# A two-layer transformer kernel: the first token tile of layer two is transposed inside layer one's last block, the routing's reads and first norm are tied to the projections, and the rope's buffers are doubled

## The chip, the core and the metric

One core of a Trainium2 chip runs the whole program in one launch. The metric is the device time of that launch in microseconds, median of several runs. The engines are named as in the profile: PE (TensorE, matrix products and transposes), DVE (VectorE), ACT (ScalarE), POOL (GpSimd) and SP (SyncE, which here only issues DMAs). Each engine works through its own queue in order, and semaphores tie the queues together. A stage's tiles live in SBUF, products in PSUM.

## The reference

2048 tokens of width 512, float32 throughout. Cut to what matters:

```python
xn = layernorm(x)
x  = x + linear_attention(xn) + moe_ffn(xn)       # layer one: 16 heads; 16 experts, top 8, dense
xn = layernorm(x)
x  = x + window_attention(xn) + depth_ffn(xn)     # layer two

def window_attention(x):          # 16 heads of 32, causal window of 1024
    q, k, v = split(x @ w_qkv)
    q, k = rope(rmsnorm(q) * q_gamma), rope(rmsnorm(k) * k_gamma)
    return softmax(mask(q @ k.T / sqrt(32))) @ v @ w_out

def depth_ffn(h):                 # only 256 of the 2048 tokens are processed
    scores = h @ w_router
    idx = sort(top_k(scores, 256))
    z = h[idx]                    # gather
    a = rms_norm(z) -> q, k, v (16 heads of 128) -> rope -> causal attention -> wo
    x1 = z + a
    y = x1 + silu(rms_norm(x1) @ w_gate) * (rms_norm(x1) @ w_up) @ w_down
    h[idx] = sigmoid(scores[idx]) * y + (1 - sigmoid(scores[idx])) * z
    return h
```

## The kernel before

A token tile is 128 tokens (16 of them, t = 0 to 15), a block is 512 tokens (b = 0 to 3).

**Layer one** runs the keys of all tiles, then four blocks of experts (about 141 us each). At the end of a block four groups `po` (seven products each, L515 to L518) give the layer's output for one token tile each; VectorE adds the residual (L519) and takes the layer norm's sums. In the last block each tile is normed at once by `normed`: xn goes to the DRAM tensor `xn_d`, the router's score to `score` (L98), xn plus x to `res_d`.

**The projections of layer two** (the `with ExitStack() as p4` stage) are the place of the change. For each token tile t:
- `turned(t)` takes xn of the tile, loaded two tiles ahead from `xn_d` into `xnq` (three buffers), transposes it on PE (`tr2`, L110) into PSUM, and ScalarE copies it to `xnt` (L117, three buffers). It is called for t + 1 after the first projection of tile t; tile 0's call stands just before the loop.
- three projections p0, p1, p2 (q, k, v) of four products each (L942), into three PSUM buffers;
- `normed_qk`: ScalarE squares p0 and p1 into `t1` (L740), VectorE sums to `rr` (L741), square root and reciprocal (L78, L79), VectorE scales to `qk` (L744), and POOL makes the rope: `t1 = qk*cos` (L749), `t2 = swapped qk*sin` (two halves, L754), `qk = t1 + t2` (L759). `t1` and `t2` have one buffer, `qk` two. The last tile's rope is on VectorE;
- `turned_qk`: PE transposes q and k of the tile before (`trqk`, L110), ScalarE copies into `qT`, VectorE into `kT`.

Between the products stand the steps of `maxima` (class `Steps`, `early`): score products `pa` (L593, with masks L599 and L601) of an earlier query tile into one PSUM buffer, which VectorE reduces at once (`mx`, L605); `tn` (L618) turns the finished maxima.

**The routing** finds the 256 largest scores while the projections run. It is a generator, `routing()`, and each `next(route, None)` in the projection loop runs it to its next `yield`. `largest` finds the threshold by counting: eight steps (h0 to h3, l0 to l3), each with POOL work `thr`, `ge` (L830 to L839), one small product `pc` on PE that sums over partitions (L843), ScalarE's copy `got`, and POOL work on it (L847 to L851):

```python
yield
pc = ps_t.tile([P, 15], F32, tag="tr", name=f"pc_{name}{k}")
PE.matmul(pc, ones, ge[:, :, 0], start=True, stop=True)
got = read(pc, f"got_{name}{k}")
yield
```

Then come two prefix sums (`ties`, `place`, products L878 to L881), and sixteen scatters of (token, score) pairs by indirect DMA from POOL's queue into four lists in DRAM (`list_d`, L911, four for each quarter; the indices `place` are in tiles that share the two buffers of `rr`). The lists were cleared before by four DMAs from a zeroed tile `lists`. Once tile 13 is in the program (`gathering`), POOL reads the four lists back, adds them, casts `idx` (L925) and issues four indirect DMAs that gather the rows `xs` and their rope table (`gather`, L674).

**The depth block** follows: `rms_norm_T(xs, 0, "a")` norms the gathered rows in two halves (`hn_a`: square on ScalarE L1001, scale on VectorE L1003, transposes `trh_a` on PE), and projections `k2p`, `v2p`, `q2p` follow, with weights streamed by SP. Then come its attention, its feed-forward net and, to the end, the window attention of layer two.

The order of instructions on each engine is not the order of the source lines: a scheduler builds each queue from the dependences and its own estimates. So an instruction of a later source line, such as hn_a, can stand early in a queue where its inputs are estimated to be there. The pools' buffers decide which tiles reuse which memory, and a tile waits for the last reader of what was there.

## Time and profile before

| | |
|---|---|
| runs | 1734.67, 1738.12, 1739.71 us; median 1738.12 |
| profiled execution | 1734.86 us, span 1733.2 us |
| instructions in the profile | 20487 |
| mean granted PE clock | 0.986 |
| PE, DVE, ACT, POOL busy | 1665.0, 966.0, 588.3, 532.7 us |
| keys of layer one, 0 to 150 us | PE busy 138.2 |
| experts, 150 to 696 | PE busy 545.7 |
| last po groups, 696 to 720.3 | PE busy 24.3 |
| projections and routing, 720.3 to 1045.5 | PE busy 282.4, POOL 174.8, DVE 180.3, granted clock 0.95 |
| depth block, 1045.5 to 1350 | PE busy 296.7 |
| window attention, 1350 to 1733 | PE busy 377.7 |

How to read it: "busy" is the time in which an engine had an instruction in work; a matmul in float32 leaves two rows in the trace. In a timeline row stand the start, the length, the engine, the line, the operation and tiles; in brackets the idle time of the engine before it, and what ended that. Tile names are shown without their numbers, so `t` is t1 or t2. In a row of busy time by stage stand the stretch, its length, the busy time of PE, PE's weight loads, DVE, ACT and POOL (each with its count), the granted PE clock as a share of full speed, the share of the DMA engines, and GB/s.

### The profile page before, as it was taken

The page shows a single profiled execution, that of the slowest core. Times are in us where ns is not written, and L with a number is a line of the kernel's source. Part 1 is how long each engine was busy: PE and PEld are TensorE (multiplying, and loading weights), DVE is VectorE, ACT ScalarE, POOL GpSimd, SP SyncE. Part 2 cuts the span into 40 slices and gives each one's busy share as a digit, 9 for nine tenths or more (in the row PEclk, how much of TensorE's full clock was granted, in tenths as well). Part 3 has the DMA queues.
Part 4 walks back from the last instruction along what each step waited for, and adds up shares of the span by engine and source line. Part 5 has one row for each costly group of instructions (what it writes and reads, how often), then busy time and mean ns, then how long its engine had stood idle before and what let it go on. Part 6 is the DMA issues. An engine that isn't in the chain of part 4 may idle for free.

```text
span 1733.2 us, 20487 instructions
## 1 busy us (share of the span) xinstructions
PE 1665.0 (96%) x8118; PEld 748.8 (43%) x8118; DVE 966.0 (56%) x1226; ACT 588.3 (34%) x947; POOL 532.7 (31%) x500
## 2 busy tenths in 40 slices
PE   8999999999999999988979989999999999999999
PEld 3445444444444444443434334454565333433333
DVE  4755646445344543335546676686555467567465
ACT  3313334333253254121111111242100566447473
POOL 3230000000000200178663333330000577558684
PEclk9999999999999999999989999999899999999999
DMA  9401001211031231310110005212132300110101
GB/s 358 169 33 46 25 31 36 74 54 31 18 116 57 54 115 37 63 47 25 25 40 25 13 20 204 99 50 73 47 116 65 114 2 1 50 50 1 50 1 37
DMA packets 61808, 107.11 MB, mean 62 GB/s; under 512 B 12208, under 2 KB 13744, under 8 KB 61200
## 3 DMA queue, kind: packets, MB, share of 16 engines
q1 hardware_dynamic: 55280, 104.01, 18.1%
q0 software_dynamic: 1152, 1.21, 0.5%
q10 hardware_dynamic: 5280, 0.59, 0.4%
q8 instruction: 63, 1.03, 0.2%
q14 instruction: 33, 0.27, 0.1%
HBM read 84.14 MB, written 21.65 MB: 61 GB/s over the span
## 4 chain that ended last, share of the span: by engine, by line
PE 80%; DVE 8%; POOL 5%; issue 2%; ACT 2%; DMA 2%; SPq 0%; POOLq 0%; DVEq 0%; ACTq 0%
PE ea L493 6%; PE eg L491 6%; PE acc L477 6%; PE ps L1271 6%; PE pa L593 6%; PE av L1345 5%; PE p L942 5%; PE po L515 3%; PE pq L366 3%; PE po L1315 3%; PE gx L241 3%; DVE mx L605 2%; PE mg L1185 2%; PE q2p L1017 2%; PE mu L1189 2%
## 5 line engine op out<-in xcount | busy, mean ns | idle before, releaser
L605 DVE TENSOR_REDUCE mx<-pa 128x4 f32<-128x1536 f32 (+3 forms) x144 | 253.1, 1757 | 157.6 <-PE pa L601 75.1
L1378 POOL TENSOR_TENSOR acc<-acc,pt 128x1024 f32<-128x1024 f32 (+2 forms) x110 | 252.6, 2325 | 95.7 <-DVE acc L1378 44.7
L1305 ACT ACTIVATE pt<-ps 128x1024 f32<-128x1024 f32 (+3 forms) x208 | 181.4, 924 | 107.9 <-PE ps L1294 61.6
L1378 DVE TENSOR_TENSOR acc<-acc,pt 128x1024 f32<-128x1024 f32 (+1 forms) x80 | 143.4, 1820 | 103.7 <-POOL acc L1378 103.7
L593 PE MATMUL pa<-kT,qT 32*128 32x384 f32 (+3 forms) x1152 | 139.3, 545 | 22.4 <-DVE mx L605 22.1
L349 ACT ACTIVATE r_e<-eg 128x512 f32<-128x512 f32 x128 | 75.8, 594 | 202.2 <-PE eg L491 194.4
L1271 PE MATMUL ps<-qT,kT 32*128 32x512 f32 (+3 forms) x1152 | 139.0, 525 | 0.0
L720 POOL TENSOR_TENSOR cosg<-cosg,gam 128x512 f32<-128x512 f32 x2 | 2.5, 1264 | 442.7 <-DVE gam L717 442.7
L942 PE MATMUL p<-w_qk,xnt 128*128 128x512 f32 x256 | 132.1, 639 | 3.9 <-ACT xnt L117 3.9
L351 DVE TENSOR_TENSOR h<-ea,r_e 128x512 f32<-128x512 f32 x128 | 87.3, 685 | 82.7 <-ACT r_e L350 82.2
L491 PE MATMUL eg<-xl,rwgT 128*128 128x512 f32 x256 | 130.8, 592 | 0.0
L493 PE MATMUL ea<-xw,rw1T 128*128 128x512 f32 x256 | 130.8, 592 | 0.0
L477 PE MATMUL acc<-h,rw2T 128*128 128x512 f32 x256 | 129.3, 592 | 0.0
L1345 PE MATMUL av<-pt,v 128*32 128x512 f32 (+3 forms) x1024 | 100.8, 482 | 0.0
L1271 PEld LDWEIGHTS ps<-qT,kT 32*128 32x128 f32 x1152 | 54.7, 183 | 93.8 <-issue 65.7
L593 PEld LDWEIGHTS pa<-kT,qT 32*128 32x128 f32 x1152 | 46.6, 187 | 105.4 <-DVE mx L605 67.2
L487 DVE TENSOR_TENSOR xw<-xw,xl 128x512 f32<-128x512 f32 x64 | 43.8, 686 | 84.9 <-DMA xw<-w_d 84.7
L350 ACT ACTIVATE r_e<-r_e 128x512 f32<-128x512 f32 x128 | 80.3, 629 | 5.6 <-ACT r_e L349 1.8
L491 PEld LDWEIGHTS eg<-xl,rwgT 128*128 128x128 f32 x256 | 48.7, 190 | 61.2 <-issue 60.5
L493 PEld LDWEIGHTS ea<-xw,rw1T 128*128 128x128 f32 x256 | 48.7, 190 | 61.2 <-issue 58.8
L477 PEld LDWEIGHTS acc<-h,rw2T 128*128 128x128 f32 x256 | 48.6, 190 | 61.2 <-issue 54.2
L942 PEld LDWEIGHTS p<-w_qk,xnt 128*128 128x128 f32 x256 | 46.4, 203 | 43.5 <-issue 39.5
(339 smaller groups left out, 2458.0 us busy)
## 6 DMA issues: line engine op xcount, KB each, us to landing
xw<-w_d SPq DMA_DIRECT2D x64, 256.0 KB, 3.3
x<-in_x SPq DMA_DIRECT2D x16, 256.0 KB, 4.5
res_d<-x SPq DMA_DIRECT2D x16, 256.0 KB, 3.5
xr<-res_d SPq DMA_DIRECT2D x16, 256.0 KB, 4.6
xn_d<-xn SPq DMA_DIRECT2D x16, 256.0 KB, 3.0
res_d<-xr SPq DMA_DIRECT2D x16, 256.0 KB, 3.3
xnq<-xn_d SPq DMA_DIRECT2D x16, 256.0 KB, 2.7
v_d<-vt SPq DMA_DIRECT2D x16, 256.0 KB, 2.0
```

Of the source, the lines that this page charges most:

```text
L350: S.activation(r, r, AF.Square)
L351: V.tensor_tensor(dst, pa, r, ALU.mult)
L477: PE.matmul(acc, rw2T[:, j, e, :], h, start=e == 0 and j == 0, stop=e == E - 1 and j == 1,)
L491: PE.matmul(pg, rwgT[:, e, hb], xl, start=True, stop=True)
L493: PE.matmul(pa, rw1T[:, e, hb], xw, start=True, stop=True)
L593: PE.matmul(pS[:, h, : w * P], qT[r, g, i * P : (i + 1) * P], kT[r, g, ks], start=True, stop=not (edge or last),)
L605: V.tensor_reduce(mx[:, g, :, c], pS[:, :, : w * P], AX.X, ALU.max)
L942: PE.matmul(pj, xnt[:, c, :], w, start=c == 0, stop=c == NC - 1)
L1271: PE.matmul(pS[h // 2][:, h % 2, t0 * P - q0 : (t1 + 1) * P - q0], kT[r, g, kb * P : (kb + 1) * P], qT[r, g, t0 * P : (t1 + 1) * P], start ...
L1305: S.activation(pT[:, :, :n], pS[hp][:, :, :n], AF.Exp)
L1345: PE.matmul(self.av[h * HD : (h + 1) * HD, t0 * P - o : (t1 + 1) * P - o], vs[kb // 4][:, kb % 4, hs], got[h // 2][:, h % 2, t0 * P - q0 : ...
L1378: eng.tensor_tensor(part, part, got[hp][:, :, : q1 - q0], ALU.add)
```

## The change

Five edits, all around the projections of layer two.

1. The pools for the projections' inputs (`w4`, `xq`, and a pool `xt4` of its own for `xnt`) are opened inside the last block of layer one, after the region of layer one's `xnT` is closed. `turned(0, ps, "mm")` is called there, ahead of the last token tile's po group, with a PSUM buffer of layer one.
2. `t1` and `t2` of the rope have two buffers each.
3. `next(route, None)` is called in the middle of each of the three projections and after each (six times for a tile, four before), and a count has one `yield` more between `ge` and its product.
4. The clearing DMAs read a small tile `empty`. `lists`, and two new small tiles `tok` and `nil`, are taken from the pool of `xnt`, so that each waits for the last reader of an older `xnt`: the list reads wait for tile 9's projections, the index (through `tok`) for tile 12's, and `zero` (through `nil`) for tile 13's.
5. The squares of `rms_norm_T` take `zero` as their bias.

```diff
-        xp = l0.enter_context(tc.tile_pool(name="xp", bufs=1, side="right"))
+        xp = xp_in.enter_context(tc.tile_pool(name="xp", bufs=1, side="right"))
...
+                if b == NTB - 1:
+                    xp_in.close()
+                    def pool(name, bufs):
+                        return p4.enter_context(
+                            tc.tile_pool(name=name, bufs=bufs, side="right", reuse_waits="tile")
+                        )
+                    w4, xq, xt4 = pool("w4", 1), pool("xq", 3), pool("xt4", 3)
...
+                    def turned(t, pool, tag):
+                        xn = xnq.pop(t)
+                        if t + 2 < NT:
+                            load_xn(t + 2)
+                        xnt = xt4.tile([P, NC, P], F32, tag="xnt", name=f"xnt_{t}")
+                        transpose4(
+                            pool, lambda c: xn[:, c * P : (c + 1) * P], xnt, f"tr2_{t}", scopy, tag
+                        )
+                        return xnt
+                    load_xn(0)
...
+                    load_xn(1)
...
+                    if t == NT - 1:
+                        xnt = turned(0, ps, "mm")
                     po = mm(f"po_{b}_{i}")
...
-            t1 = wka.tile([P, 2, HEADS, HD], F32, tag="t1", name=f"t1_{t}", bufs=1)
+            t1 = wka.tile([P, 2, HEADS, HD], F32, tag="t1", name=f"t1_{t}")
...
-            t2 = wka.tile([P, 2, HEADS, HD], F32, tag="t2", name=f"t2_{t}", bufs=1)
+            t2 = wka.tile([P, 2, HEADS, HD], F32, tag="t2", name=f"t2_{t}")
...
-            lists = const([P, 4, 2, 2], "lists", r5)
-            G.memset(lists, 0.0)
+            empty = const([P, 2, 2], "empty", r5)
+            G.memset(empty, 0.0)
...
                     yield
+                    yield
                     pc = ps_t.tile([P, 15], F32, tag="tr", name=f"pc_{name}{k}")
...
-            while not gathering:
+            while len(gathering) < 1:
                 yield
+            lists = xt4.tile([P, 4, 2, 2], F32, tag="xnt", name="lists")
...
-            G.tensor_copy(idx, listed[:, :, 0])
+            while len(gathering) < 2:
+                yield
+            tok = xt4.tile([P, 2], F32, tag="xnt", name="tok")
+            G.tensor_copy(tok, listed[:, :, 0])
+            G.tensor_copy(idx, tok)
...
+            while len(gathering) < 3:
+                yield
+            nil = xt4.tile([P, 1], F32, tag="xnt", name="nil")
+            G.memset(nil, 0.0)
+            G.tensor_copy(zero, nil)
             yield
...
-        xnt, last_qk = turned(0), None
+        last_qk = None
...
                     if c == 1:
                         early.some(t - 1)
-                        if j == 1 and t > 0:
+                        if t > 0:
                             next(route, None)
...
-                    next_xnt = turned(t + 1)
+                    next_xnt = turned(t + 1, ps_t, "tr")
+                    if t + 1 in (NT - 5, NT - 2, NT - 1):
+                        gathering.append(t)
...
-                S.activation(h, src[:, j, :], AF.Square, accum_out=ss)
+                S.activation(h, src[:, j, :], AF.Square, bias=zero, accum_out=ss)
```

The order of the queues that the two programs are built to differs in these places. PE: tr2 of tile 0 stands before the last po group; the counts pc of h1, h3, l1 and l3 stand at the end of p0 and no longer in the middle of p1, those of h0, h2, l0 and l2 in the middle of p2 and no longer at its end; ties stands before p2 of tile 5 and no longer after it, place at the end of p2 of tile 5 and no longer in the middle of p1 of tile 6. ACT and DVE: the first half of hn_a stands after the last trqk and no longer after tile 8. POOL: twelve scatters stand before the rope of tile 6 and no longer eight, the last four before the rope of tile 7 and no longer after it; the list reads follow the rope of tile 9 and no longer precede that of tile 8, the gather that of tile 12. SP: the loads of xnq for tiles 3 and 4 stand a few places earlier, and the biases `k2b` with the weights `k2w`, whose memory is now that of older q and k tiles.

## The prediction

> **What bounds the kernel now.** I read the page's first line, then the busy time by stage, then TensorE's waits inside the one stage that is not full.

> ```profile
> PE 1665.0 (96%) x8118; PEld 748.8 (43%) x8118; DVE 966.0 (56%) x1226; ACT 588.3 (34%) x947; POOL 532.7 (31%) x500
> 696.00:720.30 24.30, 24.30 (x59) 10.75 (x58) 9.34 (x27) 3.91 (x7) 0.00 (x0) 1.00 0.17 65
> 720.30:1045.50 325.20, 282.36 (x1328) 125.99 (x1326) 180.34 (x202) 58.86 (x123) 174.76 (x250) 0.95 0.14 35
> ```

> TensorE is the bound, and every edit lies around 720.3 to 1045.5, the projections of layer two. There it idles 325.2 - 282.4 = 42.8 us, at a granted clock of 0.95. Only idle time and clock there can be won. TensorE's timeline shows where (start, length, instruction, then the idle before it and who ended it):

> ```profile
> 724.60 5.40 PE L942 MATMUL p<-w_qk,xnt 128*128 128x512 f32 x8 [3.85 <-ACT xnt L117]
> 746.44 0.63 PE L110 MATMUL trqk<-ident,qk 128*128 128x128 f32 x4 [1.53 <-ACT xnt L117]
> 762.77 0.40 PE L843 MATMUL pc_h<-ge_h,ones 128*128 128x15 f32 x2 [3.56 <-POOL ge_h L839]
> 783.71 0.61 PE L843 MATMUL pc_h<-ge_h,ones 128*128 128x15 f32 x2 [2.84 <-POOL ge_h L839]
> 804.27 0.40 PE L843 MATMUL pc_l<-ge_l,ones 128*128 128x15 f32 x2 [1.77 <-POOL ge_l L839]
> 823.25 0.39 PE L843 MATMUL pc_l<-ge_l,ones 128*128 128x15 f32 x2 [2.25 <-POOL ge_l L839]
> 868.22 1.09 PE L110 MATMUL trqk<-ident,qk 128*128 128x128 f32 x4 [4.74 <-ACT xnt L117]
> 907.73 1.66 PE L593 MATMUL pa<-kT,qT 32*128 32x384 f32 x8 [8.23 <-DVE mx L605]
> ```

> Four of the eight are pc, the routing's count. The last names VectorE, but the chain of waits shows its origin, the gather of the chosen rows:

> ```profile
> 900.76 3.46 DMA xs<-xn_d,idx
> 904.24 0.73 ACT hn_a L1001 x2
> 905.52 0.49 DVE hn_a L1003
> ```

> hn_a, the norm of the gathered rows, stands in the ACT and DVE queues at token tile 8, so the projections' own work waits behind the gather.

> **A wait costs twice.** After 3.85 us of idle, eight rows of p took 5.40 us instead of 3.60 (as at 730.27): 1.8 more. The same comparison gives 1.9 after 3.56, 1.8 after 2.84, 2.0 after 2.25, 2.2 after 4.74, 2.7 after 8.23, and nothing after 1.53 and 1.77. So I add 2.0 to a wait above 2 us. [...]

> **Removed.**
> - Transpose of token tile 0 (tr2, then xnt's copy) now stands before the last po group. TensorE has something ready at 720.8: 3.85 + 1.8 = 5.65 us. Its four transposes (0.44) and ScalarE's copy (0.57) only move; ScalarE sits idle 3.95 us before 716.01, which covers the copy. The new t1 waits for the store of the last res_d rows (issued 724.10, landing 2.1 later); its second half needs p1 at 728.3, so nothing.
> - Two buffers for t1 and t2. ScalarE's squares no longer wait for POOL's rope of the tile before. The 1.53 at 746.44 becomes 0.5 (then rope itself is late): 1.0. The 4.74 at 868.22 has the same form: squares and xnt's copy wait for a rope held behind eight scatters. In the new order twelve scatters (1.27 us apart) precede that rope, which ends 28.3 us after the place matmul: 1.8 to the index copy, three trains of 5.1 with two starts of 0.8 and 0.5, one landing of 3.8 less 1.3, and 7.25 of rope. TensorE has 31.1 us of work and slow clock to issue first (28.6 from the rows 834.3 to 863.5, less the place itself, 0.45, and 2.0). So the wait is gone, 2.9 us in hand: 4.74 + 2.2 = 6.9.
> - hn_a behind the last tile: 8.23 + 2.7 = 10.9. Gather and list reads sit on POOL after ropes 12 and 9. Four list reads, landing and adds take about 7 us, gather with its copies 5.5; POOL is idle 9.66 us between ropes there (928.29 to 937.96), so neither delays a rope.

> Together 5.65 + 1.0 + 6.9 + 10.9 = 24.45 us.

> **Added: the counts come earlier in TensorE's queue.** The extra yields move each second count (h1, h3, l1, l3) from the middle of p1 to the end of p0. That is 1.72 us of p plus a transpose and a maxima step less ahead of it, and as much more behind it. TensorE issues in order, so a count that is early waits with everything behind it. The ring: count, rest of p1, squares to qk, rope, count chain, next such count. From POOL's timeline:

> ```profile
> 791.66 2.35 POOL L749 TENSOR_TENSOR t<-qk,cosg 128x1024 f32<-128x1024 f32 x1 [0.76 <-DVE qk L744]
> 793.98 2.51 POOL L754 TENSOR_TENSOR t<-qk,sing 128x512 f32<-128x512 f32 x2
> 796.56 2.35 POOL L759 TENSOR_TENSOR qk<-t,t 128x1024 f32<-128x1024 f32 x1
> 802.79 1.43 POOL L839 TENSOR_TENSOR ge_l<-ge_l 128x120 f32<-128x120 f32 x4
> ```

> From 791.66 to the count at 804.27 is 12.6 us; interleaved as in the new order 12.4. From p1's end to the rope's start is 4.35 (806.32 to 810.65). From count to p1's end is now 5.4 of work for l1 (p 3.6, transpose, one maxima step, the count) plus 2.0 of clock. Ring l1 to l3: 12.4 + 7.4 + 4.35 = 24.15, where it was 804.27 to 823.25 = 19.0. TensorE has 16.3 + 2.0 us in it, so it waits 5.85. Likewise h3 to l1: 12.4 + 8.2 + 4.35 = 24.95 against 19.9 of work: 5.0. h1 to h3: 9.6 to the next count, 0.7 to read it, 12.7 of chain and rope = 23.0 against 16.7: 6.3. For h1 the chain restarts at 742.6 and takes 10.1 with a rope in it; TensorE arrives at 749.2: 3.45. Last, the place matmul stands at the end of p2 and not in the middle of the next p1: l3 to place is 7.6 + 4.35 + 10.35 = 22.3 against 16.15: 6.15, where it waited nothing. Sum: 3.45 + 6.3 + 5.0 + 5.85 + 6.15 = 26.75, plus 1.9 + 4 x 2.0 of clock = 36.65. Before: 3.56 + 2.84 + 1.77 + 2.25 + 1.9 + 1.8 + 2.0 = 16.1. Added: 20.5.

> **At the end of the stage**, both halves of hn_a follow the last tile; the first meets the transposes and maxima there, 0.3. The first weight of the next stage now reuses memory that holds qk until the last trqk: it is issued at 1041.2, not 1038.17. With landings of 5.2 (q2w) to 6.3 (k2w) it arrives 0.3 to 1.4 after TensorE asks; a queued one (v2w, 9.8) would give 5. I take 0.6, so 0.9 for the end. The biases beside it, the small tile that resets the lists, the zero tile and its use as bias: nothing; POOL's gaps and the queue behind that weight hide them, at 0.2 each if not.

> **Sum**: -24.45 + 20.5 + 0.9 = -3.0. The profiled execution took 1734.86 (span 1733.2 and 1.7 around it), 3.3 under the median; on the median of 1738.1 that is 1735.1. The difference of two sums of 20 is not known better than about 6 us: five clock losses of 1.4 to 2.7 each, 1 us in each ring.

> **Rivals.**
> 1. *The counts wait no more than before.* If POOL or the copies around it run freer (rope no longer starts late in tile 2, the steps interleave), the 20.5 does not arise: -24.45 + 0.9 = -23.5; with the scatter wait of 6.9 kept, -16.7, or 1721.4. For it: POOL is idle 4.13 and 2.34 us before two of the old ropes. Against: 4.35 + 12.4 is a chain without slack.
> 2. *VectorE gets between.* In the rings the reduction of a maxima step (1.67 to 2.21 us) stands just ahead of rr, the sum that starts the rope. It ends about as p1 does. If it begins over 0.5 us late, it pushes the rope: up to 2.2 us in each of four rings, 8.8, with TensorE idle all of it: 1735.1 + 8.8 = 1743.9, slower.
> 3. *The handover isn't won.* Should the early transposes wait, or ScalarE's copy fall behind the norm of the last rows, 5.65 returns: 1740.8.

> **Chances.** Forecast 0.50, its own range 1729 to 1742: 0.14 of it below, 0.30 within and 0.06 above the 0.3% (5.2 us) that a measurement can tell from no change. Rival 1 0.27, faster. Rival 2 0.17, slower. Rival 3 0.06, 0.04 within and 0.02 slower. Faster 0.14 + 0.27 = 0.41, same 0.34, slower 0.25. The range goes from rival 1 with its scatter wait, less 1.4, to rival 2 plus 2.1: 1720 to 1746.

> **What would show it.** Right: no wait at the first p of tile 0; none at trqk of tile 6; hn_a after the last trqk and no DMA in front of a pa; waits of 5 to 6.5 us before pc_h, pc_l and place, and 23 to 25 us between them. Wrong: counts that wait under 3 us (rival 1), a pc released late because a rope began over 5 us after p1's end (rival 2), or a wait at k2p above 2 us.

## The result, and the profile after

| kernel | median us | ratio to before, 95% interval |
|---|---|---|
| before | 1735.45 (12 runs beside the change) | |
| changed | 1735.43 (12 runs) | 0.9998 [0.9989, 1.0007] |

No difference that can be measured. The profiled execution took 1737.09 us (span 1735.1, mean granted clock 0.985). The page's first line and two stages by the same cut as before:

```profile
PE 1668.9 (96%) x8118; PEld 750.4 (43%) x8118; DVE 965.6 (56%) x1226; ACT 589.8 (34%) x947; POOL 532.6 (31%) x503
696.00:720.30 24.30, 24.30 (x61) 10.97 (x60) 9.33 (x27) 4.50 (x8) 0.00 (x0) 1.00 0.21 76
720.30:1045.50 325.20, 285.95 (x1321) 127.70 (x1319) 179.41 (x201) 59.66 (x122) 174.52 (x253) 0.94 0.11 30
```

TensorE is busy 1668.9 us instead of 1665.0 with the same 8118 instructions, and idle 1735.1 - 1668.9 = 66.2 instead of 68.2. The idle time did fall, by 2.0; the same products took 3.9 longer. Most of that is the granted clock: half of TensorE's busy time inside the stage's stretches at half clock, which is what they cost (in the changed kernel four rows of p took 3.73 us at half clock, from 779.04, and 1.94 at full clock, from 784.17), is 13.3 us before and 16.2 now. This execution is the slowest of the changed kernel's 12, so the profiles differ by more (1.9 us of span) than the medians do (0.0). TensorE's timeline shows what became of the eight rows of before (start, length, then the idle time before it in brackets):

```profile
721.03 3.60 PE L968 MATMUL p<-w_qk,xnt 128*128 128x512 f32 x8
739.87 0.66 PE L110 MATMUL trqk<-ident,qk 128*128 128x128 f32 x4 [0.33 <-POOL qk L772]
752.36 0.40 PE L857 MATMUL pc_h<-ge_h,ones 128*128 128x15 f32 x2 [2.67 <-POOL ge_h L852]
774.74 0.61 PE L857 MATMUL pc_h<-ge_h,ones 128*128 128x15 f32 x2 [5.53 <-POOL ge_h L852]
802.51 0.61 PE L857 MATMUL pc_l<-ge_l,ones 128*128 128x15 f32 x2 [4.34 <-POOL ge_l L852]
827.37 0.61 PE L857 MATMUL pc_l<-ge_l,ones 128*128 128x15 f32 x2 [5.75 <-POOL ge_l L852]
844.94 0.40 PE L892 MATMUL place<-sel,after 128*128 128x16 f32 x2 [0.96 <-POOL sel L910]
849.35 0.61 PE L893 MATMUL place<-inc,ones 128*128 128x16 f32 x2 [4.01 <-POOL inc L889]
881.22 0.60 PE L110 MATMUL trqk<-ident,qk 128*128 128x128 f32 x4
1046.97 1.98 PE L1043 MATMUL k2p<-k2w,hT_a 128*128 128x512 f32 x4 [0.47 <-DMA k2w<-in_wk]
```

The first p of tile 0 has no wait in front (3.85 before), nor has trqk of tile 6 at 881.22 (4.74), and no gather stands before a pa (8.23). In their place the second counts and place wait 2.67 + 5.53 + 4.34 + 5.75 + 0.96 + 4.01 = 23.3 us, where the counts waited 10.4.

### The profile page after: what moved, and what is told of

Read it like the earlier page. It is cut to its first block, busy times and chain, and to the rows that moved or that the text cites. A ratio compares the mean times of both kernels' runs of the same rounds, so it can differ in the third digit from the quotient of the medians.

```text
span 1735.1 us, 20506 instructions
## 1 busy us (share of the span) xinstructions
PE 1668.9 (96%) x8118; PEld 750.4 (43%) x8118; DVE 965.6 (56%) x1226; ACT 589.8 (34%) x947; POOL 532.6 (31%) x503
## 4 chain that ended last, share of the span: by engine, by line
PE 81%; DVE 8%; POOL 4%; DMA 2%; issue 2%; ACT 2%; SPq 0%; DVEq 0%; POOLq 0%; ACTq 0%
PE ea L494 6%; PE acc L478 6%; PE eg L492 6%; PE p L968 6%; PE pa L632 6%; PE ps L1297 6%; PE av L1371 5%; PE po L553 3%; PE pq L367 3%; PE po L1341 3%; PE gx L242 3%; DVE mx L644 2%; PE mg L1211 2%; PE q2p L1043 2%; PE sg L403 2%
## 5 line engine op out<-in xcount | busy, mean ns | idle before, releaser
L288 PE MATMUL pk<-k_wT,xnT 128*128 128x512 f32 x128 | 61.6, 624 | 3.5 <-ACT xnT L117 3.5
```

## Experiments

All are timed beside before, in three groups, where its medians were 1736.96, 1736.02 and 1735.77 us. The differences told below are taken from the ratios (0.9893 is 0.0107 x 1736 = 18.6 us); some expectations name those of the medians, which are up to 1.5 us apart from them. Each kernel has one trace.

| kernel | edits in it | median us | ratio to before, 95% interval |
|---|---|---|---|
| early transposition alone | 1 | 1729.02 | 0.9963 [0.9949, 0.9976] |
| two buffers alone | 2 | 1723.41 | 0.9931 [0.9918, 0.9945] |
| cadence alone | 3 | 1758.42 | 1.0131 [1.0116, 1.0147] |
| ties alone | 4, 5 | 1725.40 | 0.9937 [0.9923, 0.9950] |
| edit 3 undone | 1, 2, 4, 5 | 1718.43 | 0.9893 [0.9877, 0.9910] |
| edit 2 undone | 1, 3, 4, 5 | 1738.82 | 1.0020 [1.0010, 1.0029] |
| ties undone | 1, 2, 3 | 1734.85 | 0.9995 [0.9986, 1.0004] |
| edits 1 and 2 | 1, 2 | 1716.16 | 0.9887 [0.9872, 0.9902] |
| waits filled | all, and filling | 1729.94 | 0.9964 [0.9950, 0.9978] |
| slow cadence | 1, 2, 4, 5, half of 3 | 1704.39 | 0.9815 [0.9801, 0.9828] |
| slow cadence, ties undone | 1, 2, half of 3 | 1704.34 | 0.9820 [0.9807, 0.9834] |
| slow cadence, even scatters | as slow cadence, and more | 1699.32 | 0.9790 [0.9777, 0.9804] |

**Edit 3 undone.** The question: did the counts take back what the rest won, or was nothing won?

```diff
-                        if t > 0:
+                        if j == 1 and t > 0:
                             next(route, None)
...
-                    yield
                     yield
                     pc = ps_t.tile([P, 15], F32, tag="tr", name=f"pc_{name}{k}")
```

> Changed kernel with edit 3 undone (one call of next in the middle of a tile's projections, not three; one yield before a count's product): edits 1, 2, 4 and 5 stand alone. Theory T (the counts' waits and the half clock behind them took back what the other edits won): in the trace of the changed kernel the second counts and place wait 2.67 + 5.53 + 4.34 + 5.75 + 0.96 + 4.01 = 23.3 us and the slow clock behind them takes about 14.3, where before had 16.1 in all; so 21.5 us go: 1735.4 - 21.5 = 1714, between 1709 and 1719, with waits of 1.5 to 4 us before pc and none before place. Rival R1 (nothing was won: TensorE idles in this stage for whatever comes late next, and the counts only took the place of other waits): 1731 to 1737, and waits of 20 us or more before other products. Rival R2 (the two-buffer rope or the gather isn't worth its part): 1720 to 1726.

It is 18.6 us faster than before, interval 15.6 to 21.4: R1 falls. TensorE's waits (us in total, times, longest):

```profile
PE pc_h L856 <- POOL ge_h L852: 6.1, 2, 3.5
PE pc_l L856 <- POOL ge_l L852: 4.1, 2, 2.3
PE trqk L110 <- POOL qk L772: 3.3, 2, 3.0
```

The counts wait 10.2 and place nothing. But 1718.4 is 4.4 above the 1714 expected: with the old cadence trqk of tile 6 still waits 3.0 us, now for the rope itself, behind eight scatters.

**Cadence alone** (edit 3 put into before).

> Kernel before with edit 3 alone (three calls of next in the middle of a tile's projections, two yields before a count's product). Theory T: the second counts come early and wait 23 to 27 us with 10 to 14 of slow clock behind, where they cost 16.1 before: +20.5 to +21.5; with one buffer for t1 and t2, twelve scatters instead of eight stand before the rope that the squares of the next tile wait for, at most 5 more: 1735.5 + 21 = 1756.5, between 1752 and 1763. Rival R1 (the stage has a fixed amount of idle time): 1733 to 1742, the waits of the gather and the scatters shrinking by what the counts wait more.

22.7 us slower, interval 20.1 to 25.5, as theory T has it. Its waits, and the pa behind the gather:

```profile
PE pc_l L844 <- POOL ge_l L839: 10.1, 2, 5.8
PE pc_h L844 <- POOL ge_h L839: 8.2, 2, 5.6
PE place L880 <- POOL inc L876: 4.0, 1, 4.0
913.77 1.67 PE L593 MATMUL pa<-kT,qT 32*128 32x384 f32 x8 [9.31 <-DVE mx L605]
```

The counts wait as in the changed kernel, and the gather's wait did not shrink to make room (9.31, it was 8.23). One thing was not expected: with single buffers and twelve scatters before the rope of tile 6 there is no wait at trqk of tile 6. Place stands earlier there, and TensorE has more to issue before that trqk; the next experiment but one tests whether the edit and not the buffers removes the wait.

**Early transposition alone** (edit 1).

> Changed kernel with edits 2, 3, 4 and 5 undone: the early transposition of tile 0 alone. Theory T: the idle 3.85 us before the first p of tile 0 and 1.8 of slow clock go, 5.65 in all: 1735.5 - 5.65 = 1729.9, between 1727.5 and 1732. Rival R3 (the first counts take it back: their chain starts at the last scores of layer one, so TensorE only reaches pc_h0 and pc_h1 earlier and waits there): within 1.5 us of 1735.5, with a wait of 6 us or more before pc_h1, where it was 3.56.

6.4 us faster, interval 4.2 to 8.9: R3 falls. The first p starts at once, and trqk of tile 6 still waits:

```profile
720.43 3.60 PE L956 MATMUL p<-w_qk,xnt 128*128 128x512 f32 x8
860.69 1.09 PE L110 MATMUL trqk<-ident,qk 128*128 128x128 f32 x4 [4.55 <-ACT xnt L117]
```

The wait before pc_h1 is the 3.56 us it was. Beyond the handover, two other waits are shorter: 2.28 before h3 (2.84) and 0.66 before l1 (1.77). Why these two shift a little from kernel to kernel wasn't followed up.

**Edit 2 undone, and two buffers alone.** Both change only `bufs=1` of t1 and t2.

> Changed kernel with edit 2 undone (one buffer each for t1 and t2), the rest as it is. The kernel with edit 3 alone has single buffers and yet no wait before trqk of tile 6, since place comes earlier there. Theory T2 (that wait is removed by edit 3, not by the buffers, which are worth only the 1.53 us before trqk of tile 0): 1735.4 + 1.2 = 1736.6, between 1735 and 1739, no wait before trqk of tile 6. Rival (the prediction's own ledger, buffers worth 1.0 + 6.9): 1743.3, with a wait of 3 us or more before trqk of tile 6.

> Kernel before with edit 2 alone (two buffers each for t1 and t2). Theory T2: with the old cadence the rope of tile 6 is itself late behind eight scatters; the kernel with edit 3 undone waits 2.98 us there for qk: 1.53 becomes 0.34 and 4.74 becomes 2.98, together 3.0, the slow clock behind the wait stays: 3 us faster than before, between 1.5 and 5. Rival (the prediction's own term): 7.9 faster, 6 or more, and no wait before trqk of tile 6.

Undone, it costs 0.22%, 3.8 us, against the changed kernel; neither 7.9 nor quite 1.2. Its rows show where:

```profile
740.89 0.63 PE L110 MATMUL trqk<-ident,qk 128*128 128x128 f32 x4 [1.53 <-ACT xnt L117]
756.34 1.11 PE L110 MATMUL tr<-ident,xnq 128*128 128x128 f32 x4 [2.15 <-ACT got_h L117]
884.08 0.63 PE L110 MATMUL trqk<-ident,qk 128*128 128x128 f32 x4 [0.88 <-ACT xnt L117]
```

Only 0.88 us at trqk of tile 6; but a wait of 2.15 behind the copy of a count, which no expectation had listed. ScalarE's queue holds that copy behind a square that waits for the rope (idle 9.82 us until POOL's qk):

```profile
755.62 0.60 ACT L753 ACTIVATE t<-p 128x512 f32<-128x512 f32 x1 [9.82 <-POOL qk L772]
756.12 0.17 ACT L117 COPY got_h<-pc_h 128x15 f32<-128x15 f32 x1
```

Alone, the two buffers bring 12.0 us (9.5 to 14.2) where 3 were expected. That was wrong by much, and the rows say why. The wait at tile 6 is still there, but the norm of the gathered rows has moved (second row, ScalarE):

```profile
866.11 0.66 PE L110 MATMUL trqk<-ident,qk 128*128 128x128 f32 x4 [3.60 <-POOL qk L759]
1028.55 0.63 ACT L1001 ACTIVATE hn_a<-xs 128x512 f32<-128x512 f32 x1
```

In before hn_a runs at 904.2, in the middle of tile 8's work. With two buffers the scheduler puts it behind the last tile, though no line of code asks for that, and the 8.23 us go with it. What in the scheduler's estimates moved it was not looked into.

**Ties alone, ties undone, edits 1 and 2.** So edits 2 and 4 may remove the same wait. Three kernels test that.

> Kernel before with edits 4 and 5 alone (the small tiles come from the buffers of xnt in its own pool). Theory T: the 8.23 us before the pa of tile 9 and 2.7 of slow clock go, 0.3 come back at the end of the stage: 10.6 faster than before, between 8.5 and 12.5; hn_a stands behind tile 15's xnt. Rival R6 (the wait only moves: the gather now ends behind tile 14, and rr of tile 14 or 15 waits behind hn_a): at most 6 faster, with a wait of 3 us or more before a pa or a trqk of tiles 14 and 15.

> Changed kernel with edits 4 and 5 undone (edits 1 to 3 stay). Edit 2 alone had already moved hn_a behind the last tile, with no wait before the pa of tile 9. Theory T3 (edits 2 and 4 each remove the same 8.23 + 2.7 us, so the second is worth nothing): within 2 us of the changed kernel, 1735.4, no wait above 3 us before a pa. Rival (the prediction's ledger, 10.9 by edits 4 and 5): 1746, a wait of 8 us before a pa near tile 9.

> Kernel before with edits 1 and 2 only (edits 3, 4 and 5 undone). Theory T3: the two alone moved the time by -7.9 and -12.6; the rope that is late behind the scatters stays, so their sum and the kernel with edit 3 undone (1718.4) should meet: 1717, between 1713 and 1720. Rival: edits 4 and 5 add 10.9 to it in the kernel with edit 3 undone, so without them 1725 to 1730.

Alone, the ties bring 10.9 us (8.7 to 13.4), hn_a's first half runs late, and no pa waits over 1.9 us (R6 falls):

```profile
998.03 0.72 ACT L1012 ACTIVATE hn_a<-xs,zero 128x512 f32<-128x512 f32 x1
```

Beside edit 2 they bring nothing: without them the changed kernel takes 1734.85 (ratio 0.9995, against 0.9998), and edits 1 and 2 alone (0.9887) do as well as edits 1, 2, 4 and 5 (0.9893). T3 holds: edits 1, 2 and 4 with 5 bring 6.4 + 12.0 + 10.9 = 29.3 us each by itself and 18.6 together, and the 10.7 between are the one wait that two of them remove.

**Waits filled.** Is the slow clock behind the waits caused by them?

```diff
-                    pc = ps_t.tile([P, 15], F32, tag="tr", name=f"pc_{name}{k}")
+                    pc = ps_t.tile([P, D], F32, tag="tr", name=f"pc_{name}{k}")
+                    for _ in range({'h1': 2, 'h3': 5, 'l1': 4, 'l3': 5}.get(f"{name}{k}", 0)):
+                        PE.matmul(pc, ident, w_v[:, 0, :], start=True, stop=True)
+                    pc = pc[:, 0:15]
```

(and four such products ahead of place).

> Changed kernel with idle time filled: ahead of the counts h1, h3, l1, l3 and of place stand 2, 5, 4, 5 and 4 products of 128x512 (0.86 us each) of ident with w_v, written to the count's own PSUM tile and overwritten by it. Theory T (the half clock behind the waits is caused by the idle time, and lengthens the rings themselves): the waits before these products fall from 23.3 to under 8 us in all, the granted clock between 740 and 860 us from 0.83 to 0.90 towards 1.0, and of the 14.3 us of slow clock 8 to 14 go, 1 to 3 us of the filling not covered: 1725, between 1720 and 1730. Rival R7 (the half clock comes of something else than TensorE's idle time): 1735 to 1745, clock as before, the filling partly added.

A kernel with 18.0 us of additional products is 0.34% faster, 5.9 us, than the changed kernel without them. Busy time and clock from 740 to 860 us, the changed kernel first, then this one:

```profile
740.00:860.00 120.00, 95.31 (x428) 45.54 (x429) 46.35 (x59) 19.48 (x44) 79.72 (x163) 0.86 0.07 20
740.00:860.00 120.00, 112.99 (x506) 52.57 (x504) 50.46 (x63) 21.39 (x47) 83.05 (x165) 0.97 0.10 23
```

The clock rises from 0.86 to 0.97 as the idle time falls from 24.7 to 7.0 us, and place is issued 7.5 us earlier (841.84 against 849.35). So the slow clock comes of the idle time (R7 falls), and it lengthened the rings: p1 stands in each of them. Of the 7.5 a new wait took back 3.1, and VectorE shows whose it is:

```profile
857.52 1.22 DVE L754 TENSOR_REDUCE rr<-t 128x32 f32<-128x1024 f32 x1 [3.35 <-DMA list_d<-tokc,place]
861.40 0.93 PE L632 MATMUL pa<-kT,qT 32*128 32x384 f32 x8 [3.10 <-DVE mx L644]
```

`place` shares the two buffers of rr, so rr of a tile waits until a scatter has read its indices, here 3.35 us.

**Slow cadence.** The calls of next as before (four for a tile), the two yields of the change kept. A count now takes three calls, so it stands one call further behind its `ge` than with edit 3 undone, and the counts come every 0.75 tile and not every half. The expectation's "1.33 tiles" has the fraction upside down.

> Changed kernel with the calls of next as before (four for a tile), but with the two yields before a count's product kept: a count comes every 1.33 tiles and not every half or whole one. Theory T: a ring from one count to the next is 22 to 28 us with a rope in it and about 10 without, and TensorE has 1.33 tiles, 24 us or more, of work between two counts: waits of under 3 us in all before pc and place, so that also the 16.1 us that the counts cost before go: 1714 - 13 = 1701, between 1696 and 1707; the gather comes some 40 us later, still ahead of the last tile's end. Rival R4 (POOL's queue, not the place of the counts, sets when they end; slower calls only move the waits): 1711 to 1718, like the kernel with edit 3 undone. Rival R5 (the later gather is late for hn_a): a wait of over 3 us before trh_a at the end of the stage.

> The kernel with four calls of next for a tile and two yields before a count's product (1704.4), with edits 4 and 5 undone: are they needed where the counts no longer wait? Theory T3: hn_a stays behind the last tile, nothing waits for the gather: 1704.4, between 1702 and 1707; two list reads now stand before the rope of tile 10 and two inside it, at most 2 us. Rival (they are needed): 1712 or more, with hn_a's gather ahead of a pa.

1704.4 with the ties and 1704.3 without: R4, R5 and the need for the ties fall. The counts' waits are down to 0.91 us in all. The time expected was met, but not for the reason given: there are 9.9 to 15.6 us between two counts and not 24. What the rows show is that `ge` is ready when TensorE arrives: POOL's last add of it ends 3.0 to 9.5 us before the product for h1, h3 and the four l counts, and only h2 waits. What is left is one rope late behind scatters, seen in POOL's rows and in TensorE's:

```profile
870.05 0.19 POOL L923 CAST place<-pos 128x4 int32<-128x4 f32 x1 [3.06 <-DMA list_d<-tokc,place]
875.51 2.37 POOL L762 TENSOR_TENSOR t<-qk,cosg 128x1024 f32<-128x1024 f32 x1
882.81 1.07 PE L110 MATMUL trqk<-ident,qk 128*128 128x128 f32 x4 [2.26 <-POOL qk L772]
```

**Slow cadence, even scatters.**

```diff
-                for _ in range(4):
+                for _ in range((6, 4, 3, 2)[n]):
                     yield
```

> The kernel with four calls of next for a tile and two yields before a count's product, and with 6, 4, 3 and 2 yields behind the four groups of scatters where each had 4. Four scatters then stand before the ropes of tiles 8, 9, 10 and 11 and not eight before that of tile 8; list reads and gather stay where they are. In the trace with 4 yields each the rope of tile 8 began 8.1 us later than its qk, after 3.06 us in which POOL waited for a scatter's landing, since place and rr share two buffers, and TensorE waited 2.26 us at trqk of tile 8, with 3.41 us of half clock behind. Theory T4: this wait and its slow clock go: 1704.4 - 4.0 = 1700.4, between 1698 and 1703. Rival R8 (the wait moves to a later tile, or into rr, whose buffers wait for later scatters): 1703 to 1707 with a wait of 2 us or more before a trqk or a pa of tiles 9 to 12.

1699.3, the fastest of all: 2.1% under before, interval 1.96 to 2.23%. T4 holds, R8 falls. The rope of tile 8 starts as soon as its qk is there, and the page gives the least busy time of any:

```profile
867.07 2.35 POOL L762 TENSOR_TENSOR t<-qk,cosg 128x1024 f32<-128x1024 f32 x1 [0.56 <-DVE qk L757]
PE 1654.2 (97%) x8118; PEld 744.3 (44%) x8118; DVE 965.4 (57%) x1226; ACT 589.2 (35%) x947; POOL 533.8 (31%) x503
```

## Why the prediction came out as it did

The time of 1735.43 lies 0.3 us from the 1735.1 forecast, but that is closer than the working was, and luck: it subtracted 3.0 from a median of 1738.12 out of three runs; beside the change before ran at 1735.45, and the change moved the time by 0.0. That two sums of over 20 us nearly cancel was right, though the chances put faster (0.41) above same (0.34). Of the two sums the traces and experiments say this:

- **Handover, 5.65.** Right: no wait at the first p, 6.4 [4.2, 8.9] alone, of which 1.7 are the two other waits that were shorter there. Rival 3 did not come.
- **Two buffers, 1.0 and 6.9.** In the changed kernel both waits are gone, as said (0.33 at tile 0 where 0.5 was predicted, none at tile 6). But the 6.9 was put down to the wrong edit. The earlier place matmul removes that wait, with single buffers too (0.88 left); two buffers under the old cadence leave 3.0 to 3.6 of it. The argument of 28.3 us of scatters and rope (its terms add up to 28.15) against 31.1 us of TensorE's work held, with less in hand: the rope ends 30.3 us after place's second product (849.35 to 879.69), and TensorE comes to trqk after 31.9 (881.22). In before it came there 19.6 us after place (843.84 to 863.48) and waited 4.74. The 31.1 came from the early place, which was booked as a cost alone.
- **Gather and hn_a, 10.9.** The size is right (10.9 alone), and it is gone. It could have been had from edit 2 alone, and so edits 4 and 5 are worth nothing here. The prediction compared the queues of before and after only, and these cannot tell which edit moved an instruction.
- **Counts, 26.75 of waits.** 23.3 measured: 2.67, 5.53, 4.34, 5.75 and 4.97 for 3.45, 6.3, 5.0, 5.85 and 6.15. Rivals 1 and 2 are out. The rings h1 to h3 and l1 to l3 came as predicted (22.4 and 24.9 for 23.0 and 24.15). Ring h3 to l1 took 27.8 and not 24.95: from h3 to the end of p1 TensorE needed 11.4 us instead of 8.2, at half clock, while rope and count took 12.2 (12.4 predicted). VectorE did not come between: in all four rings rr starts 0.7 us after p1's end, and the rope follows 4.2 us after it, but for the ring from h1 to h3, where POOL's own count chain holds it back (5.8).
- **Slow clock, 2.0 for each wait above 2 us.** This is the step that failed. By it the change should have saved 6.7 of slow clock at the removed waits and cost 9.9 - 5.7 = 4.2 at the counts, 2.5 less busy time in all; the page shows 3.9 more, a miss of 6.4 us. Counted as half of the busy time at half clock, the removed waits had cost 6.5, as booked, and the counts 5.0 before. But behind the five new waits it is 1.7 (h1), 4.7 (h3), 2.7 (l1), 2.2 (l3) and 3.2 (place), 14.5 in all where 9.9 was booked. Against this miss idle time fell 2.0 where the ledger had 0.6; so the profiled execution came out 1.9 longer and not 3.0 shorter. The medians miss by 3.0, since the profiled pair is wider apart than they are. The windows around h3's wait show the form that the loss has:

```profile
770.40:773.81 3.41, 0.00 (x0) 0.00 (x0) 0.00 (x0) 0.00 (x0) 3.41 (x4) 1.00 0.00 0
773.81:777.22 3.41, 2.48 (x10) 1.72 (x10) 0.00 (x0) 0.17 (x1) 1.90 (x10) 0.50 0.00 0
777.22:780.64 3.42, 3.42 (x12) 1.69 (x11) 1.23 (x1) 0.58 (x1) 2.81 (x8) 0.50 0.30 77
780.64:784.05 3.41, 3.41 (x13) 1.04 (x12) 0.00 (x0) 0.00 (x0) 1.07 (x4) 0.50 0.02 5
784.05:787.46 3.41, 3.41 (x15) 1.90 (x14) 1.91 (x2) 1.07 (x2) 0.00 (x0) 1.00 0.00 0
```

One window without a matmul (second column: PE busy; third from the right: granted clock), then three windows at half clock, although TensorE was busy through the last two. 2.48 + 3.42 + 3.41 = 9.3 us of work ran at half speed, a loss of 4.7 where 2.0 was booked. In before each count that lost clock had one window at half clock behind it; here they have 1, 3, 2, 2 and 2.
- **End of the stage, 0.9.** 0.6 measured: from the last trqk to k2p 6.0 us (1040.95 to 1046.97) where it was 5.4 (1040.49 to 1045.87), with 0.47 of wait for k2w where 0.6 was taken. The profiled execution is thus 0.5 late at that trqk and 1.1 late at k2p; the other 0.8 of its 1.9 arise after k2p, where of the edits only the bias of edit 5 is left.

By experiment the other edits save 18.6 us together and edit 3 costs (0.9998 - 0.9893) x 1736 = 18.2 beside them. The ledger had 24.45 less 0.9 at the stage's end, 23.5, and 20.5. The larger miss, 4.9 in what is saved, is about the wait at tile 6: with the old cadence it still stands (3.0 us and one window of half clock behind it), so the edits that were credited with it don't remove it, and edit 3 does, which makes its own bill smaller.

## What to carry to other kernels

Put a product that waits for another engine's chain so far down TensorE's queue that the chain has ended when TensorE arrives: here counts and a place that stood half a projection earlier cost 18 us, and counts one call further behind their chains, a quarter of a tile further apart, won 13.5 (0.9893 to 0.9815). Book a removed wait once, and test each edit alone and left out: here edits that brought 6.4, 12.0 and 10.9 alone brought 18.6 together. A queue that two tiles share through their buffers (place and rr, scatters and ropes) is a wait in hiding, and here it showed as soon as the wait ahead of it went: 3.35 us of VectorE with the waits filled, 3.06 of POOL and 2.26 of TensorE with the slow cadence.

## What the runs showed of the hardware

What decided, by these two traces, is TensorE's busy share in one window, counted here over the windows of 700 to 1060 us that ran at full clock. Of 11 with a busy share of 0.42 or less, all 11 were followed by half clock; of 6 between 0.455 and 0.485, 2; of 170 above, none. So 2.0 us of idle time inside one window were enough (share 0.42, from 862.06 us in before), and the 1.77 us before l1, which fell across two windows in before (1.53 and 0.24), cost nothing there. The way back is less sure: in the same stretch TensorE was busy throughout in 13 windows at half clock, and after 12 of them the clock was full; the other stands behind h3 in the changed kernel (777.22), and what sets it apart stays open. Since the phase differs between the two (the same stretch begins at 978.11 us in one and at 978.61 in the other), the price of a wait between 2.0 and about 4.0 us (an estimate: one to two times that idle time) is in part chance.
